# Gate stage as one stream of 8-row blocks, basic block with its bands prepared in stages

## The chip, the cores and the metric

The kernel runs on one core of a Trainium2 chip. The metric is the device time of one execution in microseconds (us); the kernel before takes 7872.17 us, the median of three runs (7866.06 to 7881.12). All data is 32-bit float.

## The reference

Input x has the shape (2, 128, 128, 128): two images (B = 2), 128 channels, 128 rows (H), 128 columns. Four layers follow each other:

- **Layers 0 and 2**: a 3x3 convolution, a small state-space scan (Mamba) over eight tokens of 16 channels at each pixel, a group normalisation, SiLU, and the layer's input added.
- **Layer 1, the density gate**, which the change touches. For each 8x8 window, channel c in a group of 32 gets a density from its distances to the group's channels, then a small network turns the densities into gains, and the gains are interpolated to all pixels:

```
dist(c, d) = |x_c - x_d|^2 over the 64 pixels of the window, c and d in one group
den(c)     = mean over d of exp(-dist / 2)
hid        = relu(w1 den + b1)            # 128 -> 32 channels, one value a window
gain       = 0.5 + sigmoid(w2 hid + b2)   # 32 -> 128 channels, one value a window
out        = x * bilinear_upsample(gain)  # 16x16 windows -> 128x128 pixels, corners aligned
```

- **Layer 3, the basic block**, which the change also touches: relu(x + bn2(conv3x3(relu(bn1(conv3x3(x)))))), with the batch statistics taken over both images, so that each normalisation waits for a whole convolution.

## The kernel before, in words

Channels lie on the 128 partitions. Layers 0 and 2 (`_mamba`) run in an order written out by hand, in which every operation has a due time. They fill 0 to 3320 us and 3640 to 6950 us and are not changed. SiLU and the residual of layer 0 are made at the beginning of the gate stage, those of layer 2 at the beginning of the basic block.

**Gate stage, `_gates`** (3320 to 3640 us). Each image has 16 blocks of 8 rows (`nh`), 32 blocks in all. A block goes through these steps:

- `load`: y and the layer's input, SiLU on ScalarE (L636), residual on GpSimd (L638) into x, window by window.
- `turn`: eight PE transposes (L652) into PSUM (`pt`), copied by VectorE to xt (L654), squared by ScalarE to xq (L656); ScalarE squares x (L659) and VectorE sums the squares per window to nsq (L661, L662).
- `density`: 72 small matmuls, each two instructions (L671, L681), then kk on VectorE (L689), a minimum with 0 on GpSimd (L695), Exp on ScalarE (L696).
- `total`: sums kk (L700).
- `gain`, once for each image after its 16 blocks: two small matmuls, Relu, Sigmoid, + 0.5.
- `apply`: the upsampling as matmuls over 32 rows of contraction (L738), multiplied by x on VectorE (L747), stored from ScalarE's queue (L751).

An image's applies come only after its `gain`, so x of a whole image is held in SBUF (`nh + 5` buffers). The PSUM tiles of turn, gain and apply share two buffers of three banks (`wide`). The order of this stage's instructions is left to the framework's scheduler.

**Basic block, `_basic_block`** (6946 to 7861 us). The 3x3 convolution goes over 32 bands of 8 rows. Four combinations of a band's rows (`combine`: two on GpSimd, L818 and L821, two on VectorE, L819 and L820) are multiplied by transformed weights, which takes twelve matmuls of 512 columns a band, 24 PE instructions (L828). ScalarE copies one product (L836); VectorE forms the two output rows (L839 to L842) and takes statistics (L844). `convolve` prepares one band ahead:

```
v = combine(band(*bands[0]))
for k, at in enumerate(bands):
    ahead = combine(band(*bands[k + 1])) if k + 1 < len(bands) else None
    conv(u, v, *at, stats)
    v = ahead
```

In the first convolution `first` loads a band and the layer's input, applies SiLU (L876), adds the residual on GpSimd (L877) and stores the result, x3, from ScalarE's queue (L878). In the second, `second` takes the rows from SBUF (L900) and copies the two rows that bands share (L894). A closing pass loads x3 (L910), adds (L911), applies Relu (L912) and stores (L913), with three buffers in rotation.

Of the kernel before, what the change touches and what calls it, by code (L numbers as in the profile page):

```python
# [24 lines left out]
F32 = mybir.dt.float32  # L25
# [66 lines left out]
def _place(k):  # L92


    q = k // 2
    return k % 2 + 2 * (q // 4), q % 4


def _upsampling(H):

    _, fy = _bilinear(H)
    ix, fx = _bilinear(P)
    wx = np.zeros((P // WIN, P), np.float32)
    wx[ix, np.arange(P)] = 1.0 - fx
    wx[ix + 1, np.arange(P)] += fx
    segs = _segments(H)
    up = np.zeros((4, 2, P // WIN, 4, max(e - a for _, a, e in segs), P), np.float32)
    for k, a, e in segs:
        n, g = _place(k)
        for h in range(a, e):  # L110
            up[g, 0, :, n, h - a] = (1.0 - fy[h]) * wx
            up[g, 1, :, n, h - a] = fy[h] * wx
    return up.reshape(P, 4, -1)
# [488 lines left out]
def _gates(tc, src, w, con, y, stats, wm, b1, up, dst, H):  # L602

    nc = tc.nc
# [3 lines left out]
    nwin = nh * nw  # L608
    segs = _segments(H)
    with tc.tile_pool(name="dg", bufs=2) as dp, tc.tile_pool(name="dg1", bufs=1) as sp, tc.tile_pool(  # L610
        name="ps_t", bufs=2, space=PSUM
    ) as pst, tc.tile_pool(name="ps_g", bufs=1, space=PSUM) as psg:

        def wide():
            return pst.tile([P, 3 * ROWS, P], F32, tag="pt", name="pt")

        class Small:


            def tile(self, shape, dtype, tag=None, name=None):  # L620
                return wide().rearrange("p a b -> p (a b)")[: shape[0], : shape[1]]

        norm = [_norm(nc, sp, Small(), w, con, stats, b) for b in range(B)]
        ct = sp.tile([P, 4, up.shape[2]], F32, tag="ct", name="ct")

        dens = [sp.tile([P, nh, 2, npair], F32, tag=f"dens{b}", name="dens") for b in range(B)]
        held, live, gains = {}, {}, {}

        def load(b, y0):

            rows = slice(y0 * WIN, (y0 + 1) * WIN)
            g = dp.tile([P, WIN, P], F32, tag="g", name="g", bufs=4)
            nc.sync.dma_start(out=g, in_=y[b][:, rows, :])
            xr = dp.tile([P, WIN, P], F32, tag="xr", name="xr", bufs=4)
            nc.sync.dma_start(out=xr, in_=src[b][:, rows, :])
            nc.scalar.activation(g, g, AF.Silu, bias=norm[b][1], scale=norm[b][0])  # L636
            x = held[b, y0] = dp.tile([P, nw, WIN, WIN], F32, tag="x1", name="x1", bufs=nh + 5)
            nc.gpsimd.tensor_tensor(by_row(x), by_row(xr, False), by_row(g, False), ALU.add)  # L638
# [6 lines left out]

        def turn(b, y0):

            x = held[b, y0].rearrange("p x r w -> p (x r w)")

            pt = wide()[:, :npair, :]  # L650
            for k in range(npair):
                nc.tensor.transpose(pt[:, k, :], x[:, k * P : (k + 1) * P], con["ident"])  # L652
            xt = dp.tile([P, npair, P], F32, tag="xt", name="xt")
            nc.vector.tensor_copy(xt, pt)  # L654
            xq = dp.tile([P, npair, P], F32, tag="xq", name="xq")
            nc.scalar.activation(xq, pt, AF.Square)  # L656

            sq = dp.tile([P, nw, WIN * WIN], F32, tag="sq", name="sq", bufs=1)
            nc.scalar.activation(sq.rearrange("p x r -> p (x r)"), x, AF.Square)  # L659
            nsq = dp.tile([P, nw], F32, tag="nsq", name="nsq")  # L660
            nc.vector.tensor_reduce(nsq, sq, AX.X, ALU.add)  # L661
            nc.vector.tensor_scalar_mul(nsq, nsq, -0.5)  # L662
            live[b, y0] = xt, xq, nsq

        def density(b, y0):
            xt, xq, nsq = live.pop((b, y0))
# [21 lines left out]
            kk = dp.tile([P, 2, npair, CG], F32, tag="kk", name="kk", bufs=3)  # L688
# [8 lines left out]
            live[b, y0] = kk  # L697

        def total(b, y0):
            nc.vector.tensor_reduce(dens[b][:, y0], live.pop((b, y0)), AX.X, ALU.add)  # L700

        def gain(b):

            den = sp.tile([P, nh, npair, 2], F32, tag="den", name="den")
            nc.vector.tensor_scalar_mul(den, dens[b].rearrange("p y a k -> p y k a"), 1.0 / CG)
            p1 = wide().rearrange("p a b -> p (a b)")[:CG, :nwin]
            nc.tensor.matmul(p1, lhsT=wm["w1"], rhs=den.rearrange("p y k a -> p (y k a)"), start=True, stop=True)
            hid = sp.tile([CG, nwin], F32, tag="hid", name="hid")
            nc.scalar.activation(hid, p1, AF.Relu, bias=b1)
            p2 = wide()[:, :4, :]  # L710
            gt = gains[b] = sp.tile([P, 4, P], F32, tag="gain", name="gain")
            for n in range(4):
                at = (n % 2 + n // 2 * WIN) * nw
                m = min(P, nwin - at) // 32 * 32
                if m <= 0:
                    continue
                nc.tensor.matmul(p2[:m, n, :], lhsT=hid[:, at : at + m], rhs=wm["w2"], start=True, stop=False)
                nc.tensor.matmul(p2[:m, n, :], lhsT=wm["one"][:, :m], rhs=wm["b2"], start=False, stop=True)
                nc.scalar.activation(gt[:m, n, :], p2[:m, n, :], AF.Sigmoid)
                nc.vector.tensor_scalar_add(gt[:m, n, :], gt[:m, n, :], 0.5)  # L720

        def apply(b, y0):

            r0 = y0 * WIN
            pu = wide()
            o = dp.tile([P, WIN, P], F32, tag="g", name="o", bufs=4)
            x = by_row(held.pop((b, y0)))

            cut = [a for k, a, _ in segs if k % 2 == 0 and r0 < a < r0 + WIN]
            at = 0  # L730
            for first, end in zip([r0, *cut], [*cut, r0 + WIN]):
                for r in range(first, end, ROWS):
                    for k, a, e in segs:
                        lo, hi = max(a, r), min(e, r + ROWS, end)
                        if lo < hi:
                            n, g = _place(k)
                            q = slice(g * 32, (g + 1) * 32)
                            nc.tensor.matmul(  # L738
                                pu[:, at + lo - first : at + hi - first, :],
                                lhsT=gains[b][q, n, :],  # L740
                                rhs=ct[q, n, (lo - a) * P : (hi - a) * P],
                                start=True,
                                stop=True,
                                tile_position=(q.start, 0),
                            )
                rows = slice(first - r0, end - r0)
                nc.vector.tensor_tensor(  # L747
                    by_row(o[:, rows, :], False), by_row(pu[:, at : at + end - first, :], False), x[:, rows], ALU.mult
                )
                at += (end - first + ROWS - 1) // ROWS * ROWS  # L750
            nc.scalar.dma_start(out=dst[b][:, r0 : r0 + WIN, :], in_=o)  # L751

        order = [(b, y0) for b in range(B) for y0 in range(nh)]
        N = len(order)
        ready = []
        for n in range(-4, N + 2):
            if ready:
                apply(*ready.pop(0))
            if n % 2 == 0:
                for i in range(n + 4, min(n + 6, N)):  # L760
                    load(*order[i])
            if n == -4:
                nc.sync.dma_start(out=ct, in_=up)
            if 0 <= n < N:
                turn(*order[n])
            if 1 <= n <= N:
                density(*order[n - 1])
            if n >= 2:
                b, y0 = order[n - 2]
                total(b, y0)  # L770
                if y0 == nh - 1:
                    gain(b)
                    ready += [(b, i) for i in range(nh)]
        for at in ready:
            apply(*at)


def _basic_block(tc, src, y, norm, x3, w1, w2, bn, out, B, H):
# [6 lines left out]
    with tc.tile_pool(name="bb", bufs=1) as cp, tc.tile_pool(name="bband", bufs=2) as bp, tc.tile_pool(  # L785
# [28 lines left out]
        def combine(xb):  # L814

            v = combined()
            d = [xb[:, k : k + BAND - 1 : 2, :] for k in range(4)]
            nc.gpsimd.tensor_tensor(v[:, 0], d[0], d[2], ALU.subtract)  # L818
            nc.vector.tensor_tensor(v[:, 1], d[1], d[2], ALU.add)  # L819
            nc.vector.tensor_tensor(v[:, 2], d[2], d[1], ALU.subtract)  # L820
            nc.gpsimd.tensor_tensor(v[:, 3], d[1], d[3], ALU.subtract)  # L821
            return v
# [32 lines left out]
        def rest():  # L855
            return bp.tile([P, BAND + 2, P], F32, tag="xs", name="xs", bufs=3)

        bands = [(b, r0) for b in range(B) for r0 in range(0, H, BAND)]

        def convolve(u, band, n):  # L860

# [134 lines left out]
```

## Time and profile before

The profiled execution has a span of 7860.9 us.

| stage | from, us | to, us |
|---|---|---|
| layer 0 without its SiLU and residual | 0 | 3320 |
| gate stage (table load of the first SiLU to the end of the last apply) | 3332.4 | 3634.5 |
| layer 2 without its SiLU and residual | 3640 | 6950 |
| basic block: weights and first bands | 6946 | 6980 |
| basic block: first convolution | 6980 | 7390 |
| basic block: second convolution | 7401 | 7733 |
| basic block: closing pass | 7741 | 7861 |

| engine | busy, us | share of the span |
|---|---|---|
| PE (matmul) | 6537.9 | 83% |
| PEld (weight load) | 2217.4 | 28% |
| DVE (VectorE) | 6831.1 | 87% |
| ACT (ScalarE) | 4291.8 | 55% |
| POOL (GpSimd) | 5521.1 | 70% |

How to read it: the shares are averages over stages with different limits, and layers 0 and 2 make up 84% of the span. For a change in the other two stages they say little; those stages have to be read by themselves. In the lines of the profile, `x<-xr,g` is the tile written and the tiles read; L638 is a line of the kernel before.

### The profile page before, as it was taken

The page shows a single profiled execution, that of the slowest core. Times are in us where ns is not written, and L with a number is a line of the kernel's source. Part 1 is how long each engine was busy: PE and PEld are TensorE (multiplying, and loading weights), DVE is VectorE, ACT ScalarE, POOL GpSimd, SP SyncE. Part 2 cuts the span into 40 slices and gives each one's busy share as a digit, 9 for nine tenths or more (in the row PEclk, how much of TensorE's full clock was granted, in tenths as well). Part 3 has the DMA queues.
Part 4 walks back from the last instruction along what each step waited for, and adds up shares of the span by engine and source line. Part 5 has one row for each costly group of instructions (what it writes and reads, how often), then busy time and mean ns, then how long its engine had stood idle before and what let it go on. Part 6 is the DMA issues. An engine that isn't in the chain of part 4 may idle for free. (4 is left out here: it accounts for less than half of the span.)

```text
span 7860.9 us, 86792 instructions
## 1 busy us (share of the span) xinstructions
PE 6537.9 (83%) x29412; PEld 2217.4 (28%) x29412; DVE 6831.1 (87%) x6360; ACT 4291.8 (55%) x4835; POOL 5521.1 (70%) x1810
## 2 busy tenths in 40 slices
PE   7888888888888888777888888888888888878893
PEld 2222222222222222253222222222222222223341
DVE  5999999999999999863999999999999999963454
ACT  5656666666666656482665665666656656621112
POOL 5777887777778777652777778787777777843330
PEclk8999999999999999866999999999999999979996
DMA  7999999999999999854999999999999999955204
GB/s 203 246 243 246 253 249 247 253 250 256 249 248 254 245 249 248 225 179 127 244 249 246 250 250 251 252 251 253 252 239 249 250 250 250 250 157 139 69 0 163
DMA packets 573435, 1765.42 MB, mean 225 GB/s; under 512 B 85536, under 2 KB 239680, under 8 KB 458176
## 3 DMA queue, kind: packets, MB, share of 16 engines
q1 hardware_dynamic: 530496, 1709.54, 84.0%
q10 hardware_dynamic: 42496, 50.34, 1.8%
q8 instruction: 234, 3.83, 0.2%
q14 instruction: 209, 1.71, 0.1%
HBM read 1549.82 MB, written 209.72 MB: 224 GB/s over the span
## 5 line engine op out<-in xcount | busy, mean ns | idle before, releaser
L451 POOL TENSOR_TENSOR h<-ur,bcr 128x2048 f32<-128x2048 f32 x896 | 4060.4, 4539 | 1193.2 <-DMA bcr<-sb 1006.0
L478 DVE TENSOR_TENSOR set<-set,h 128x1024 f32<-128x1024 f32 x1792 | 2193.0, 1224 | 301.6 <-ACT set L469 216.2
L479 DVE TENSOR_TENSOR r<-set,bcr 128x1024 f32<-128x1024 f32 x1792 | 2194.1, 1224 | 61.4
L469 ACT ACTIVATE set<-set 128x1024 f32<-128x1024 f32 x1792 | 1745.6, 1006 | 868.7 <-PE set L460 854.2
L483 DVE TENSOR_TENSOR h<-set,h 128x1024 f32<-128x1024 f32 x1536 | 1864.5, 1214 | 21.3 <-POOL h L451 21.2
L460 PE MATMUL set<-dt,rep 32*128 32x512 f32 x7168 | 1400.2, 674 | 96.8 <-DVE h L483 89.9
L498 PE MATMUL ys<-r,ct 128*32 128x512 f32 x7168 | 1166.1, 632 | 36.4 <-DVE r L479 36.0
L328 PE MATMUL one<-band,conv 128*128 128x512 f32 x2304 | 1085.5, 607 | 24.6 <-DMA band<-in_x_dram 12.2
L828 PE MATMUL m<-comb,u 128*128 128x512 f32 x1536 | 689.1, 610 | 88.5 <-DVE Y L842 53.2
L406 PE MATMUL one<-xc,keep 128*64 128x512 f32 x1024 | 324.6, 717 | 471.4 <-ACT xc L363 361.5
L460 PEld LDWEIGHTS set<-dt,rep 32*128 32x128 f32 x7168 | 405.2, 193 | 992.7 <-issue 466.2
L328 PEld LDWEIGHTS one<-band,conv 128*128 128x128 f32 x2304 | 408.2, 190 | 674.4 <-issue 599.2
L489 PE MATMUL ys<-t,ct 128*128 128x512 f32 x512 | 326.4, 724 | 252.4 <-DVE v L511 250.9
L357 ACT ACTIVATE xc<-one,keep 128x512 f32<-128x512 f32 x256 | 176.1, 688 | 519.5 <-PE one L355 514.7
L498 PEld LDWEIGHTS ys<-r,ct 128*32 128x32 f32 x7168 | 181.2, 111 | 928.5 <-issue 760.7
L828 PEld LDWEIGHTS m<-comb,u 128*128 128x128 f32 x1536 | 296.6, 195 | 480.3 <-issue 457.3
L426 PE MATMUL one<-prod,ct 128*128 128x512 f32 x512 | 290.3, 650 | 123.1 <-POOL prod L418 88.8
L380 POOL TENSOR_TENSOR u<-dt,xc 128x1024 f32<-128x1024 f32 x128 | 302.8, 2366 | 70.7 <-ACT dt L374 70.6
L355 PE MATMUL one<-y,w_in 128*128 128x512 f32 x512 | 343.5, 759 | 5.8 <-ACT xc L357 3.1
L469 ACT ACT_TABLE_LOAD x252 | 323.3, 1283 | 4.6
L370 PE MATMUL one<-xc,w_dt 128*128 128x512 f32 x512 | 313.5, 696 | 4.1 <-ACT bc L413 4.1
L427 ACT COPY t<-one 128x512 f32<-128x512 f32 x256 | 150.2, 587 | 301.4 <-PE one L426 301.4
(136 smaller groups left out, 5894.0 us busy)
## 6 DMA issues: line engine op xcount, KB each, us to landing
ur<-su SPq DMA_DIRECT2D x896, 896.0 KB, 11.5
bcr<-sb SPq DMA_DIRECT2D x896, 448.0 KB, 11.6
ur<-su SPq DMA_DIRECT2D x896, 128.0 KB, 11.1
su<-u SPq DMA_DIRECT2D x1024, 64.0 KB, 3.5
sb<-bc SPq DMA_DIRECT2D x256, 224.0 KB, 2.8
bcr<-sb SPq DMA_DIRECT2D x896, 64.0 KB, 10.9
y<-o SPq DMA_DIRECT2D x128, 256.0 KB, 9.2
band<-in_x_dram SPq DMA_DIRECT2D x28, 640.0 KB, 10.9
```

The source lines that it names most:

```text
L328: nc.tensor.matmul(py.rearrange("p (r w) -> p r w", r=ROWS), lhsT=w["conv"][:, tap, :], rhs=xb[:, r + kh : r + kh + ROWS, kw : kw + P], st ...
L355: nc.tensor.matmul(p, lhsT=w[("in", "z")[i]][:, g, :], rhs=s["y"], start=True, stop=True)
L406: nc.tensor.matmul(p[g * NQ * DS : (g + 1) * NQ * DS, :], lhsT=w[("xb", "xcm")[i]], rhs=s["xc"][:, g, :], start=True, stop=True,)
L451: nc.gpsimd.tensor_tensor(b, s["ur", t], s["bc", t][:, 0].unsqueeze(1).to_broadcast([P, NJ, NS]), ALU.mult)
L460: nc.tensor.matmul(a[j // 2][:, j % 2, :], lhsT=w["rep"][r, q, :], rhs=s["dt"][r, g, :], start=True, stop=True, tile_position=(r.start, 0),)
L469: nc.scalar.activation(x, x, AF.Exp)
L478: nc.vector.tensor_tensor(pt, pt, s["h", t - 1][:, js, :], ALU.mult)
L479: nc.vector.tensor_tensor(s["r", t][:, js, :], pt, s["bc", t - 1][:, 1].unsqueeze(1).to_broadcast([P, 2, NS]), ALU.mult)
L483: nc.vector.tensor_tensor(s["h", t][:, js, :], pt, s["h", t][:, js, :], ALU.add)
L489: nc.tensor.matmul(s["ys", g], lhsT=con["ident"], rhs=s["t1"][:, g, :], start=True, stop=False)
L498: nc.tensor.matmul(s["ys", g][a : a + NQ * DJ, :], lhsT=red[:, q, :], rhs=r[:, j, :], start=False, stop=(q == NQ - 1), tile_position=(0, a),)
L828: nc.tensor.matmul(m[:, i], lhsT=u[:, i, kw, :], rhs=v[:, i, :, kw : kw + P], start=(kw == 0), stop=(kw == 2),)
```

## The change

**Gate stage.** A row of gains needs only the window rows above and below it, so a block can be finished as soon as the hidden values of its neighbours are there. The change makes one stream of all 32 blocks, in which each step works on an older block: turn on block n, density on n - 1, total on n - 2, the first matmul with Relu (`hide`) on n - 3, the second with Exp (`gate`) on n - 5, the rest of the sigmoid (`gain`) and the upsampling matmuls (`spread`) on n - 6, `apply` and the store (`keep`) on n - 7. The sigmoid is made as 1 / (1 + exp(-z)), so that Exp is the only other table beside SiLU. The upsampling takes four window rows at once, 64 rows of contraction for each half of the block, with weights laid out by block (4 MB instead of 2.3 MB). PSUM tiles of turn and spread have two banks; two buffers are shared by both. The order is now that of the program, on all engines, and stores go through SyncE's queue.

**Basic block.** Bands lie in three rooms whose borders are cleared once. `convolve` loads three bands ahead, makes (SiLU and residual, or Relu) two ahead, and combines one ahead. All four combinations are on GpSimd. The closing pass rotates four buffers: two as before and the two of the combinations.

```diff
 def _gates(tc, src, w, con, y, stats, wm, b1, up, dst, H):
...
-            x = held[b, y0] = dp.tile([P, nw, WIN, WIN], F32, tag="x1", name="x1", bufs=nh + 5)
+            s["x"] = dp.tile([P, nw, WIN, WIN], F32, tag="x1", name="x1", bufs=14)
...
-            pt = wide()[:, :npair, :]
+            pt = pst.tile([P, npair, P], F32, tag="pt", name="pt")
...
+        def hide(b, y0):
+            p = psg.tile([CG, nw], F32, tag="one", name="ph")
+            nc.tensor.matmul(
+                p, lhsT=wm["w1"], rhs=live[b, y0].pop("den").rearrange("p a k -> p k a"), start=True, stop=True
+            )
+            nc.scalar.activation(hidden[b][:, y0 + 1, :], p, AF.Relu, bias=b1, scale=1.0 / CG)
+
+        def gate(b, y0):
+            s = live[b, y0]
+            p = psg.tile([P, P], F32, tag="one", name="pz")
+            h = hidden[b][:, y0 : y0 + 4, :].rearrange("p y x -> p (y x)")
+            for a in range(0, P, P // 2):
+                nc.tensor.matmul(p[a : a + P // 2, :], lhsT=h, rhs=wm["w2"], start=True, stop=False)
+                nc.tensor.matmul(p[a : a + P // 2, :], lhsT=wm["one"], rhs=wm["b2"], start=False, stop=True)
+            s["e"] = dp.tile([P, P], F32, tag="e", name="e")
+            nc.scalar.activation(s["e"], p, AF.Exp, scale=-1.0)
+
+        def gain(b, y0):
+            e = live[b, y0]["e"]
+            nc.vector.tensor_scalar_add(e, e, 1.0)
+            nc.vector.reciprocal(e, e)
+            nc.vector.tensor_scalar_add(e, e, 0.5)
+
+        def spread(b, y0):
+            s = live[b, y0]
+            pu = s["pu"] = pst.tile([P, 2 * ROWS, P], F32, tag="pt", name="pu")
+            for n in range(2):
+                q = slice(n * P // 2, (n + 1) * P // 2)
+                nc.tensor.matmul(
+                    pu[:, n * ROWS : (n + 1) * ROWS, :].rearrange("p r w -> p (r w)"),
+                    lhsT=s["e"][q, :],
+                    rhs=weights[q, y0, :],
+                    start=True,
+                    stop=True,
+                )
...
+        stages = ((0, turn), (1, density), (2, total), (3, hide), (5, gate), (6, gain), (6, spread), (7, apply), (7, keep))
+        E = mybir.EngineType
+        with tc.manual_schedule(engines={E.PE, E.Activation, E.DVE, E.Pool, E.SP}):
+            for n in range(-6, N + 8):
+                if n % 2 == 0:
+                    for m in range(max(n + 4, 0), min(n + 6, N)):
+                        load(*order[m])
+                    for m in range(max(n + 2, 0), min(n + 4, N)):
+                        residual(*order[m])
+                for lag, stage in stages:
+                    if 0 <= n - lag < N:
+                        stage(*order[n - lag])
 
 def _basic_block(tc, src, y, norm, x3, w1, w2, bn, out, B, H):
...
-            nc.gpsimd.tensor_tensor(v[:, 0], d[0], d[2], ALU.subtract)
-            nc.vector.tensor_tensor(v[:, 1], d[1], d[2], ALU.add)
-            nc.vector.tensor_tensor(v[:, 2], d[2], d[1], ALU.subtract)
-            nc.gpsimd.tensor_tensor(v[:, 3], d[1], d[3], ALU.subtract)
+            d = [xb[:, n : n + BAND - 1 : 2, :] for n in range(4)]
+            for i, (m, n, op) in enumerate(((0, 2, ALU.subtract), (1, 2, ALU.add), (2, 1, ALU.subtract), (1, 3, ALU.subtract))):
+                nc.gpsimd.tensor_tensor(v[:, i], d[m], d[n], op)
...
-            return bp.tile([P, BAND + 2, P], F32, tag="xs", name="xs", bufs=3)
+            return bp.tile([P, BAND + 2, P], F32, tag="xs", name="xs")
...
+            v = {}
+            for k in range(-3, len(bands)):
+                for ahead, f in ((3, load), (2, make)):
+                    if 0 <= k + ahead < len(bands):
+                        f(k + ahead)
+                if 0 <= k + 1 < len(bands):
+                    v[k + 1] = combine(k + 1)
+                if k >= 0:
+                    conv(u, v.pop(k), *bands[k], stats)
...
-        for b, r0 in bands:
-            xr = rest()[:, :BAND, :]
+        for k, (b, r0) in enumerate(bands):
+            if k % 2 == 0:
+                xr = rest()[:, :BAND, :]
+            else:
+                xr = combined().rearrange("p a b c -> p (a b c)")[:, : BAND * P].rearrange("p (r w) -> p r w", r=BAND)
```

## The prediction

> **What bounds the kernel now.** I read four views, in this order: busy time by stretch (cut where the timeline shows a stage begin or end), the waits, the timeline of one block, the groups by form. Columns of the first: stretch, its length, then busy time (and instructions) of PE, PEld, DVE, ACT and POOL, the granted TensorE clock, DMA share, GB/s.
>
> ```profile
> 3332.00:3448.00 116.00, 65.50 (x2592) 53.20 (x2592) 68.13 (x86) 111.28 (x106) 72.75 (x37) 0.71 0.63 218
> 3448.00:3560.00 112.00, 99.03 (x2225) 63.30 (x2225) 76.92 (x97) 66.61 (x71) 47.49 (x26) 0.69 0.39 138
> 3560.00:3635.00 75.00, 66.85 (x259) 33.45 (x259) 26.04 (x34) 4.11 (x8) 2.24 (x2) 0.51 0.29 117
> 6980.00:7390.00 410.00, 356.27 (x768) 150.19 (x767) 159.25 (x249) 61.99 (x62) 164.13 (x129) 0.95 0.49 133
> 7401.00:7733.00 332.00, 331.54 (x768) 145.55 (x766) 185.14 (x249) 55.59 (x62) 111.63 (x127) 0.99 0.00 0
> 7741.00:7860.00 119.00, 0.00 (x0) 0.00 (x0) 40.96 (x33) 36.61 (x32) 0.00 (x0) 0.50 0.79 269
> ```
>
> Rows one to three are the gate stage: 302 us from its first table load (3332.4) to the end of its last apply (3634.5), 9.4 us for each of 32 blocks. ScalarE bounds its first part (111 of 116 us), PE at half clock its last. Row four is the first 3x3 convolution: 410 us for the 768 PE instructions that the second (row five) does in 332 us, with PE busy throughout. So 78 us of it are waiting. Row six is the closing pass: no PE, DMA at 79%.
>
> Waits of the first convolution (who <- releaser: us, times, longest):
>
> ```profile
> ACT band L876 <- DMA band<-y: 237.8, 30, 16.8
> DVE Y L839 <- ACT m L836: 233.2, 30, 9.0
> ACT m L836 <- POOL band L877: 82.3, 25, 3.8
> PE m L828 <- DVE Y L842: 53.2, 25, 3.9
> PE m L828 <- DVE comb L819: 24.8, 1, 24.8
> ```
>
> PE waits for DVE; DVE waits for the copy L836; that copy stands in ScalarE's queue behind the x3 store, which waits for GpSimd's residual L877, for SiLU, for a band loaded one band ahead.
>
> For the gates I ask what may overlap. From the timeline of one block (start, length, instruction, idle before it):
>
> ```profile
> 3513.44 1.23 DVE L654 COPY xt<-pt 128x1024 f32<-128x1024 f32 x1 [1.98 <-PE pt L652]
> 3514.70 1.02 ACT L656 ACTIVATE xq<-pt 128x1024 f32<-128x1024 f32 x1 [2.93 <-DVE xt L654]
> 3515.62 1.05 ACT L659 ACTIVATE sq<-x 128x1024 f32<-128x1024 f32 x1
> ```
>
> The square xq reads the same PSUM tile as the copy xt, yet starts 0.03 us after xt's end, after ScalarE had idled 2.93 us. So the two readers are ordered, not parallel.
>
> Durations, from the groups by form of the gate stage:
>
> ```profile
> L638 POOL TENSOR_TENSOR x<-xr,g 128x1024 f32<-128x1024 f32 x32 | 75.4, 2361 | 80.9 <-DMA g<-y 40.8 <-ACT g L636 13.9 <-DVE o L747 10.5
> L695 POOL TENSOR_SCALAR kk<-kk 128x512 f32<-128x512 f32 x32 | 47.6, 1486 | 70.0 <-DVE kk L689 64.8 <-DVE gain L720 5.2
> L661 DVE TENSOR_REDUCE nsq<-sq 128x16 f32<-128x1024 f32 x32 | 38.9, 1216 | 32.6 <-ACT sq L659 31.9
> L636 ACT ACTIVATE g<-g,aff_t,aff_s 128x1024 f32<-128x1024 f32 x32 | 38.9, 1236 | 0.8 <-DMA g<-y 0.5
> L689 DVE TENSOR_TENSOR kk<-pg,nsq 128x512 f32<-128x512 f32 x32 | 22.0, 687 | 17.9 <-PE pg L681 17.5
> L700 DVE TENSOR_REDUCE dens<-kk 128x16 f32<-128x512 f32 x32 | 21.8, 680 | 8.8 <-ACT kk L696 8.8
> L696 ACT ACTIVATE kk<-kk 128x512 f32<-128x512 f32 x32 | 20.2, 630 | 25.3 <-POOL kk L695 25.1
> ```
>
> **What the Trainium skill says.** "TensorE: Matmul & The Clock Gate", specification table: ScalarE, VectorE and GpSimd queues are strict FIFO, TensorE's can only pull weight loads ahead. The trace agrees (L836 behind the x3 store), and my forecast rests on it. The same page, Part 1: the PE clock halves after an idle window of about 3.4 us and returns after a busy one. Rows one to three agree: 0.71, 0.69, 0.51. "GPSIMD Engine Reference", specification table: GpSimd shares SBUF with VectorE, and VectorE instructions with two SBUF inputs contend. The trace agrees: the combination on DVE takes 0.68 us at its quickest and 1.82 us, the median of the second convolution, beside GpSimd's.
>
> **The gates, part by part.** The new order is written by hand: in iteration n each engine's queue holds, in this order, turn(n), density(n-1), total(n-2), hide(n-3), gate(n-5), gain(n-6), spread(n-6), apply(n-7). With FIFO queues that gives a closed loop:
> - transposes T(n) on PE, then xt(n) on DVE 1.22, xq(n) on ScalarE 1.01 (ordered, see above), sq(n) behind it 1.05, nsq(n) on DVE 1.22, its scaling 0.17 (median);
> - kk(n-1) behind that on DVE 0.69, the min on GpSimd 1.49, Exp 0.63;
> - hide's Relu(n-3) behind that Exp on ScalarE. It reads 32x16; taken 0.20, from the 128x1 square root at 0.20;
> - gate(n-5) on PE: its PSUM tile has the tag "one" with a single buffer, which hide's tile holds until that Relu;
> - spread(n-6) behind gate on PE, then T(n+1) behind spread. The loop is closed.
>
> Outside PE: 1.22 + 1.01 + 1.05 + 1.22 + 0.17 + 0.69 + 1.49 + 0.63 + 0.20 = 7.7 us, and about 0.5 us for hand-overs (PE to DVE 0.25 as T to xt; the rest 0.03 to 0.09). On PE, full clock and half: T, eight transposes, 1.1 and 2.0. Gate is eight instructions; four such of L717/L718 took 1.2 us, with twice the columns; so 1.3 and 2.2. Spread is four instructions of 512 columns: 0.427 us each in the second convolution, 0.85 at half, with start-up 1.9 and 3.6. PE idles some 5 us in each loop (from the end of density to gate), so it starts cold and warms later: I take 1.6 + 1.7 + 2.9 = 6.2, between 4.3 and 7.8. The loop is 14.4 us, from 12.5 to 16.0.
>
> Density, 2.2 us, lies beside xt to nsq. SiLU of two blocks with its table load, 3.8 us every second iteration, and GpSimd's residuals, 4.7, lie beside spread, T and xt. The new reciprocal has no row of its shape; it lies between 0.22 (the tensor-scalar L720 of that shape, by its median) and five times that, an upper bound that I choose. Either way total 0.68, three gain operations and an occasional stall by GpSimd take under 3 us, beside the 4.5 us from the min to the end of gate: nothing. Sigmoid's three table loads go (3.8 us).
>
> Sum: iterations 0 to 5 have no spread; the loop there is xt to kk plus total, 6.3 us, or 10.3 with the two SiLUs: with 5 us of lead, 53. Iterations 6 to 31: 26 x 14.4 = 374. The drain, iteration 32 and six of gate and spread: 33. Together 460, against 302: **+158**. The new weights table is 4 MB instead of 2.3, ahead of the first loads; 2.3 MB landed in 8.8 us, so 6.8 more, half of it hidden behind the norm: **+3**. The row stores move from ScalarE's queue to SyncE's; behind a store waiting for apply stand loads needed two iterations later: nothing.
>
> **The basic block.** All four combinations go to GpSimd: 4 x 1.29 (its uncontended median) + residual 2.68 = 7.9 us a band, under PE's 332 / 32 = 10.4. Loading three bands ahead hides the 5.5 us landing, and SiLU, residual and x3 store come before the copy L836 needs its turn. The first convolution should then run as the second: 410 - 332 = **-78**. The second is PE-bound and stays. GpSimd's first two combinations at each start cost 2 x 1.29 instead of about 1.8: **+1.5** over both. The closing pass rotates four buffers instead of three: load 4.3, DVE 1.3, ACT 1.2, store 3.6 make about 10.5 us, /3 = 3.5 as now, /4 = 2.6; but DMA at 269 GB/s is 79% busy, so 340 GB/s caps 1.05 MB a band at 3.1. I take 3.25 for 32 bands, 104 for 119: **-15**.
>
> Net: 158 + 3 - 78 + 1.5 - 15 = +69.5; 7872 + 69.5 = 7941.
>
> **Rivals.** (A) The lags decouple the engines and the busiest bounds the stage. DVE would have 5.9 to 6.8 us a block, ACT 5.7. 32 x 6.5 + 25 for both ends is 233: -69, net -158, 7714. For it: nearly every stage reads an older block. Against: the FIFO loop above. (B) The loop closes over total and gain instead of min, Exp, Relu and gate (the "one" buffer binds less than I read), and PE stays warmer: 14.4 - 2.8 = 11.6, 26 x 11.6 + 86 = 388: +86, net about 0, 7872. Against: the single buffer in the code. (C) The gates as forecast, but the convolution keeps its waits: GpSimd at the contended 1.75 gives 9.7 us a band, and the order on ScalarE's queue still holds up L836. Gain 20 instead of 78: 7999. Against: no VectorE instruction with two SBUF inputs is left there.
>
> **How the numbers follow.** Forecast 0.56, A 0.12, B 0.15, C 0.13; the rest, 0.04, is wider still. The loop's bounds give 26 x 12.5 and 26 x 16.0, with the ends 76 to 95: 401 to 511, net 7880 to 7992. The range takes in these and B: 7860 to 7993. It leaves out A and C's upper end. Faster: A, and a third of B: 0.17. Same (within 16 us): the middle of B and the forecast's low end: 0.08. Slower: 0.75.
>
> **What would show it.** Right: applies 12 to 16 us apart in mid-stage; DVE, ACT and POOL each under 60% there; PE's gate waiting for Relu, transposes right behind spread; the first convolution at about 332 us. Wrong: DVE or ACT near 95% in the gates (A), gate starting before that block's Exp (B), or the first convolution above 370 us with L836 still waiting for GpSimd (C).

## The result and the profile after

The changed kernel takes 7986.98 us (median of four runs, 7969.65 to 8003.9) against 7876.65 us of the kernel before beside it: 1.014 times as long, 95% interval 1.011 to 1.0169. The forecast was 7941, slower; the time lies in its range (7860 to 7993).

The profiled spans, 7967.9 and 7860.9 us, differ by 107.0 us. By stages, each taken from its first to its last instruction (the last apply of the kernel before ends at 3633.6 us, not at 3634.5, which makes its gate stage 301.2 us):

| stretch | before, us | after, us | difference | forecast |
|---|---|---|---|---|
| up to the first SiLU of the gate stage | 3332.4 | 3327.9 | -4.5 | +3 |
| gate stage | 301.2 | 416.3 | +115.1 | +158 |
| from there to the first convolution (layer 2) | 3346.1 | 3339.2 | -6.9 | 0 |
| first convolution | 409.8 | 423.2 | +13.4 | -78 |
| between the convolutions | 10.6 | 12.7 | +2.1 | +1.5 (both starts) |
| second convolution | 332.5 | 332.6 | +0.1 | 0 |
| to the closing pass | 8.4 | 8.4 | -0.1 | 0 |
| closing pass | 120.0 | 107.5 | -12.5 | -15 |

Two terms of the forecast are far off, and they partly cancel: the gate stage lost 43 us less than I said, the first convolution gained nothing of its 78 us. Busy time by stretch of the kernel after (length; busy time and instructions of PE, PEld, DVE, ACT, POOL; clock; DMA share; GB/s), for the gate stage, the two convolutions and the closing pass:

```profile
3328.00:3744.00 416.00, 233.89 (x5312) 150.35 (x5312) 203.18 (x288) 173.05 (x222) 122.39 (x64) 0.64 0.32 119
7084.00:7507.00 423.00, 354.73 (x768) 149.41 (x766) 116.70 (x186) 60.28 (x61) 224.66 (x160) 0.95 0.48 127
7519.00:7852.00 333.00, 332.61 (x768) 146.16 (x768) 116.79 (x186) 54.06 (x60) 158.79 (x159) 0.99 0.01 2
7860.00:7967.00 107.00, 0.00 (x0) 0.00 (x0) 40.89 (x34) 36.51 (x32) 0.00 (x0) 0.50 0.84 294
```

In the gate stage no engine is busy for more than 56% of the time, and the DMA share is 0.32; ScalarE has fallen from 96% (111 of 116 us in the first part before) to 42%. Something other than the busiest engine sets the pace, and the timeline shows it. One iteration of the kernel after, weight loads and DMA left out:

```profile
3553.95 1.23 DVE L648 COPY xt<-pt 128x1024 f32<-128x1024 f32 x1 [4.35 <-PE pt L646]
...
3555.27 1.02 ACT L650 ACTIVATE xq<-pt 128x1024 f32<-128x1024 f32 x1 [4.93 <-DVE xt L648]
...
3556.19 1.05 ACT L653 ACTIVATE sq<-x 128x1024 f32<-128x1024 f32 x1
3557.27 1.22 DVE L655 TENSOR_REDUCE nsq<-sq 128x16 f32<-128x1024 f32 x1 [2.09 <-ACT sq L653]
...
3558.61 0.68 DVE L683 TENSOR_TENSOR kk<-pg,nsq 128x512 f32<-128x512 f32 x1
...
3559.38 1.48 POOL L689 TENSOR_SCALAR kk<-kk 128x512 f32<-128x512 f32 x1 [11.37 <-DVE kk L683]
...
3560.90 0.63 ACT L690 ACTIVATE kk<-kk 128x512 f32<-128x512 f32 x1 [3.66 <-POOL kk L689]
...
3561.43 0.25 ACT L703 ACTIVATE hid<-ph,b 32x16 f32<-32x16 f32 x1
3561.73 0.69 PE L711 MATMUL pz<-w,hid 32*64 32x128 f32 x4 [5.42 <-ACT hid L703]
...
3562.21 0.64 PE L712 MATMUL pz<-w 32*64 32x128 f32 x4
3562.79 2.08 PE L729 MATMUL pu<-up,e 64*128 64x512 f32 x4
...
3564.80 1.97 PE L646 MATMUL pt<-ct,x 128*128 128x128 f32 x8
...
3566.80 1.22 DVE L648 COPY xt<-pt 128x1024 f32<-128x1024 f32 x1 [4.35 <-PE pt L646]
```

Read from top to bottom, each line begins within 0.3 us of the end of the one above it, and the last is the first of the next block: 3566.80 - 3553.95 = 12.85 us. It is the loop of the prediction, link by link. The applies stand 12.6 to 13.1 us apart through the whole middle of the stage.

The first convolution waits as it did before. Waits of the kernel after in that stretch (who <- releaser: us, times, longest):

```profile
DVE Y L838 <- ACT m L835: 301.8, 30, 22.3
ACT band L886 <- DMA band<-y: 243.2, 29, 10.9
PEld m L827 <- POOL comb L820: 90.3, 30, 5.0
ACT m L835 <- POOL band L887: 78.9, 24, 3.3
PE m L827 <- DVE Y L841: 67.9, 26, 4.2
```

ScalarE still waits 243 us for bands that are now loaded three ahead. The timeline of one band says why (SPq and ACTq are the entries in which SyncE and ScalarE issue a DMA):

```profile
7202.99 0.37 SPq L878 DMA_DIRECT2D band<-y  x1
7208.03 1.46 ACT L886 ACTIVATE band<-band,aff_t,aff_s 128x1280 f32<-128x1280 f32 x1 [8.52 <-DMA band<-y]
7209.56 2.67 POOL L887 TENSOR_TENSOR band<-band,xs 128x1280 f32<-128x1280 f32 x1 [6.60 <-ACT band L886]
7212.19 4.64 POOL L820 TENSOR_TENSOR comb<-band 128x520 f32<-128x520 f32 x4
7212.27 0.42 ACTq L888 DMA_DIRECT2D x<-band  x1
7212.81 0.59 ACT L835 COPY m<-m 128x512 f32<-128x512 f32 x1 [3.32 <-PE m L827]
...
7216.05 10.54 PE L827 MATMUL m<-comb,u 128*128 128x512 f32 x24 [3.34 <-DVE Y L841]
7216.86 0.37 SPq L878 DMA_DIRECT2D band<-y  x1
```

Counting the instructions from the stage's first gives their bands. The load, SiLU, residual and x3 store are of band 12; the combinations behind them are of band 10, and the copy L835 of band 8. In the source, the combinations of band 10 stand ahead of the residual of band 12, and the copy of band 8 ahead of SiLU and store of band 12. The basic block is not under the hand-written order; the framework's scheduler placed them so. The room of band 13 comes free when the combinations of band 10 end (7216.83), and only then is it loaded. So one loop runs through load 5.0, SiLU 1.5, residual 2.7 and combinations 4.6: 13.8 us for this band (in mid-stage these loads stand 12.7 to 14.8 us apart), against 10.4 that PE needs (332.6 over 32 in the second convolution).

### The profile page after: what moved, and what is told of

Its sections match the earlier page's. It is cut to its first block, busy times and chain, and to the rows that moved or that the text cites. A ratio compares the mean times of both kernels' runs of the same rounds, so it can differ in the third digit from the quotient of the medians.

```text
span 7967.9 us, 87195 instructions
## 1 busy us (share of the span) xinstructions
PE 6541.0 (82%) x29648; PEld 2213.3 (28%) x29648; DVE 6745.4 (85%) x6304; ACT 4281.0 (54%) x4873; POOL 5628.9 (71%) x1879
## 5 line engine op out<-in xcount | busy, mean ns | idle before, releaser
L838 DVE TENSOR_TENSOR Y<-m,m 128x512 f32<-128x512 f32 x64 | 44.0, 688 | 528.1 <-ACT m L835 528.1
L820 POOL TENSOR_TENSOR comb<-band 128x520 f32<-128x520 f32 x256 | 298.1, 1197 | 165.3 <-PE m L827 161.9
## 6 DMA issues: line engine op xcount, KB each, us to landing
ur<-su SPq DMA_DIRECT2D x896, 896.0 KB, 11.5
```

The lines of the kernel that those rows point to most:

```text
L820: nc.gpsimd.tensor_tensor(v[:, i], d[m], d[n], op)
```

## The experiments

Times are medians; the ratio is to the kernel before, measured beside each run, with its 95% interval. The kernel before took 7869.70 us beside e1 to e4, 7881.64 beside e5 to e8 and 7858.19 beside e9.

| run | time, us | ratio | gate stage | first convolution | closing pass |
|---|---|---|---|---|---|
| e1_old_gates | 7876.36 | 1.0006 (0.9992 to 1.0019) | 302.9 | 422.2 | 107.5 |
| e2_block_in_order | 7890.95 | 1.0029 (1.0019 to 1.0038) | 414.5 | 331.7 | 106.3 |
| e3_later_two | 7950.49 | 1.0093 (1.0067 to 1.0119) | 373.8 | 422.9 | 110.1 |
| e4_old_gates_block | 7778.28 | 0.9887 (0.9865 to 0.9909) | 301.4 | 331.9 | 107.6 |
| e5_two_buffers | 7966.15 (one run) | | 413.1 | 422.7 | 107.4 |
| e8_later_one_buffer | 7985.92 (one run) | | 415.1 | 426.2 | 109.3 |
| e6_reorder | 7922.61 | 1.0050 (1.0032 to 1.0067) | 331.6 | 423.6 | 110.0 |
| e7_split_combine | 7803.61 | 0.9896 (0.9873 to 0.9919) | 305.8 | 332.4 | 109.5 |
| e9_seven_buffers | 7755.76 | 0.9864 (0.9835 to 0.9892) | 296.7 | 332.1 | 78.4 |

Stages are from each profiled execution. The unchanged layers vary from one execution to the next: the first SiLU of the gates stands between 3328 and 3362 us in the profiles of the changed kernel and of these nine. So stages say more than single totals.

**e1: the old gate stage with the new basic block.** `_gates` and its tables as in the kernel before, the rest as changed.

> The gate stage of the kernel before with the changed basic block. If the two parts add, the gate stage takes 302 us again instead of 418, and what is left of the change is a first convolution of 423 us instead of 410 and a closing pass of 108 instead of 120: 7870 to 7885, the kernel before within 0.2%. Rival: the changed block profits or suffers from the gate stage before it (clock, buffers), then over 7900 or under 7855.

Measured: 302.9 us of gates, 422.2 and 107.5 us in the block, and no difference in time. The whole loss is the gate stage's; the basic block's change is worth nothing as it stands, its lost 13 us paid by the closing pass.

**e2: the bands in program order.**

```diff
             v = {}
-            for k in range(-3, len(bands)):
-                for ahead, f in ((3, load), (2, make)):
...
+            E = mybir.EngineType
+            with tc.manual_schedule(engines={E.PE, E.Activation, E.DVE, E.Pool, E.SP}):
+                for k in range(-3, len(bands)):
+                    for ahead, f in ((3, load), (2, make)):
...
```

> The changed kernel, but the bands of both convolutions keep the program's order on every engine. Theory: in the changed kernel the framework put the residual of band k + 2 ahead of the combinations of band k on GpSimd, and SiLU and x3 store of band k + 4 ahead of the copy of band k on ScalarE, so that one loop goes through load 4.9, SiLU 1.5, residual 2.7 and combinations 4.6, 13.7 us a band. In program order the loop spans two bands and PE bounds: the first convolution 330 to 345 us instead of 423, the kernel about 85 us faster than the changed one, 7895 to 7915. Rival: GpSimd's sum or the landing of the bands is the bound in itself; then the first convolution stays above 400 us and the time near 7985.

Measured: the first convolution falls from 423.2 to 331.7 us. The time, 7890.95 us, is 4 us below the expected 7895 to 7915. Nothing but the order differs: the loads, combinations and buffers are the same. Its row by stretch, and one band of its timeline:

```profile
7102.00:7434.00 332.00, 331.73 (x768) 145.83 (x768) 116.73 (x186) 57.11 (x61) 225.78 (x161) 0.99 0.52 164
```

```profile
7258.87 0.59 ACT L835 COPY m<-m 128x512 f32<-128x512 f32 x1 [8.47 <-PE m L827]
7259.35 1.46 ACT L888 ACTIVATE band<-band,aff_t,aff_s 128x1280 f32<-128x1280 f32 x1
...
7260.94 2.68 POOL L889 TENSOR_TENSOR band<-band,xs 128x1280 f32<-128x1280 f32 x1 [3.38 <-issue]
7263.57 4.66 POOL L820 TENSOR_TENSOR comb<-band 128x520 f32<-128x520 f32 x4
...
7268.25 0.37 SPq L880 DMA_DIRECT2D band<-y  x1
```

PE is busy throughout. SiLU (L888) follows the copy with no wait for a band, and GpSimd idles 3.38 us a band, with 225.8 us of work in 332. GpSimd was not the bound, and neither was the landing of the bands.

**e3, e5 and e8: which link holds gate.** e5 gives gate's PSUM tile a tag of its own; e8 puts gate, gain, spread and apply one block later; e3 does both.

```diff
-            p = psg.tile([P, P], F32, tag="one", name="pz")
+            p = psg.tile([P, P], F32, tag="two", name="pz")
...
-        stages = (..., (5, gate), (6, gain), (6, spread), (7, apply), (7, keep))
+        stages = (..., (6, gate), (7, gain), (7, spread), (8, apply), (8, keep))
```

> The changed kernel with gate, gain, spread and apply one block later and a PSUM buffer of its own for gate. Theory: gate then waits for no Relu of its own iteration, and the loop closes over total and the gain operations instead of min, Exp, Relu and gate: about 11.3 us instead of 12.8, so 26 x 1.5 = 40 us less, one drain step more: 7940 to 7955. Rival: the loop is bound by the PSUM buffers of turn and spread alone; then it stays at 12.8 us and the time within 10 us of the changed kernel.

> The changed kernel with a PSUM buffer of its own for gate, nothing else. The prediction held that gate waits for the Relu because the two share one buffer. If that is the link, the loop falls from 12.8 to about 11.5 us. Rival: gate of block n - 5 reads the hidden values of block n - 3 anyway, which that same Relu writes; then the loop stays at 12.8 us.

> The changed kernel with gate, gain, spread and apply one block later, nothing else: gate reads only hidden values of earlier iterations, but still shares one buffer with hide. If data alone was the link, the loop falls to about 11.5 us; if buffer and data are links side by side, it stays within 0.3 us of 12.8, and only both together (11.5 us measured) help.

Measured: in mid-stage the applies stand 12.6 to 13.1 us apart with the buffer of its own (e5), except two steps of 11.5; 12.7 to 12.9 with the later lag (e8); 11.1 to 11.5 with both (e3, whose 7950.49 us lie in the expected range). So two links lie side by side, and either alone holds gate back: the shared buffer that the prediction named, and the data. Gate of block n - 5 reads the hidden values of four rows, the last of which is that of block n - 3, which the same iteration's Relu writes. The two short steps of e5 fit this: they belong to the last two blocks of the first image, for which block n - 3 is in the other image, so that no data link is left, and in both of them gate starts before that iteration's Relu (at 3561.91 and 3572.92 us, with Relu at 3567.09 and 3578.63).

The data link is one that the kernel doesn't need: in `_upsampling` the row index `y - y0 + 1` takes the values 0, 1 and 2 for all 128 rows of the image, never 3, so the weights of the fourth row are zero throughout. Gate waits for a row that is then multiplied by zero. A gate that reads three rows and has a buffer of its own should do what e3 does without the later lag; no run tried it.

With both links gone the loop closes where the expectation said, over the gain operations. Waits of e3 in mid-stage (us, times, longest):

```profile
PE pu L729 <- DVE e L721: 104.9, 24, 5.1
```

Spread, which in the kernel after came straight behind gate, now waits for the last gain operation, 24 times.

**e6: another order of the same instructions.**

```diff
-        stages = ((0, turn), (1, density), (2, total), (3, hide), (5, gate), (6, gain), (6, spread), (7, apply), (7, keep))
+        stages = ((6, gain), (0, turn), (3, hide), (1, density), (2, total), (5, gate), (6, spread), (7, apply), (7, keep))
```

> The changed kernel with the same lags, buffers and instructions in the gate stage, but another order in an iteration: gain, turn, hide, density, total, gate, spread, apply. Theory: strict queues close the loop, so order alone decides; with gain and hide ahead, their chain no longer stands behind kk and Exp, and spread need not wait for gain. By the same durations the loop becomes about 9.7 us: gate stage 320 to 335 us instead of 416, time 7885 to 7910. Rival: the sum of the work on PE and its half clock binds the stage; then the stage stays above 390 us.

Measured: the stage falls from 416.3 to 331.6 us, as expected; the loop alternates between 9.2 and 10.4 us. The time, 7922.61, is above the expected 7885 to 7910. In its profile, which is of its slowest run (7930.74), the layers 0 and 2, which are the same code, took 43 us more than in that of the kernel after (3357.2 and 3353.0 against 3327.9 and 3339.2); no run shows why. Timeline of an iteration of e6:

```profile
3544.83 0.25 ACT L703 ACTIVATE hid<-ph,b 32x16 f32<-32x16 f32 x1
...
3545.13 0.44 PE L711 MATMUL pz<-w,hid 32*64 32x128 f32 x4 [0.88 <-ACT hid L703]
...
3545.72 1.13 PE L729 MATMUL pu<-up,e 64*128 64x512 f32 x4
...
3546.30 0.69 DVE L683 TENSOR_TENSOR kk<-pg,nsq 128x512 f32<-128x512 f32 x1
...
3547.49 1.22 DVE L740 TENSOR_TENSOR o<-pu,x 128x1024 f32<-128x1024 f32 x1
3548.59 0.63 ACT L690 ACTIVATE kk<-kk 128x512 f32<-128x512 f32 x1 [3.51 <-POOL kk L689]
3548.86 1.94 PE L646 MATMUL pt<-ct,x 128*128 128x128 f32 x8 [2.01 <-DVE o L740]
```

Relu, gate and spread now come before kk and the Exp of their iteration. The loop that is left closes over a PSUM buffer: the transposes wait for apply, which frees it. That is still 30 us more than the old stage.

**e4 and e7: the old gates with the basic block in program order; in e7 two of the combinations are back on VectorE.**

```diff
-                nc.gpsimd.tensor_tensor(v[:, i], d[m], d[n], op)
+                (nc.vector if i in (1, 2) else nc.gpsimd).tensor_tensor(v[:, i], d[m], d[n], op)
```

> The gate stage of the kernel before and the basic block in program order. If both theories hold and add: 302 us of gates, 335 us for each convolution, 108 us of closing pass: 7785 to 7800, faster than both kernels by 1%. If the block's gain does not appear, 7870 to 7885.

> The gate stage of the kernel before and the basic block in program order, with two of the four combinations back on VectorE as before. If the order is what matters, PE still bounds: both convolutions at 332 us, and the time within 0.3% of the kernel with all four on GpSimd (7778). If moving them to GpSimd was needed, contention between the two engines lengthens VectorE's combinations to 1.8 us and the first convolution to over 345 us.

Measured: e4 takes 0.9887 of the kernel before, faster than both kernels and a little below its expected 7785. e7's convolutions take 332.4 and 331.6 us, and its ratio, 0.9896, lies within the interval of e4. The contention that its expectation names is there (VectorE's combinations took up to 1.79 us in the first convolution), but PE's work hides it. Here it doesn't matter which engine makes two of the combinations once the order is right.

**e9: e4 with seven buffers in the closing pass.** The rooms of the bands, idle by then, join the rotation.

```diff
-            if k % 2 == 0:
+            if k % 7 in (0, 3):
                 xr = rest()[:, :BAND, :]
+            elif k % 7 in (2, 4, 6):
+                xr = room[k % 7 // 2 - 1].rearrange("p a b -> p (a b)")[:, : BAND * P].rearrange("p (r w) -> p r w", r=BAND)
```

> The gate stage of the kernel before, the basic block in program order, and a closing pass that rotates seven buffers (two as before, the two of the combinations, the three band rooms). The prediction held that three buffers bound the closing pass by the round trip of a buffer and that with four the DMA does. If so, seven give little over four: the pass falls from 108 to 100 to 106 us and the kernel by under 8 us, 7770 to 7785. Rival: the round trip still binds with four; then seven take it below 95 us.

Measured: 78.4 us, not 100 to 106, so the rival was right: with four buffers the round trip of a buffer still bound the pass. The closing pass of e4 (four buffers; below its row, what SyncE's loads of x3 waited for) and of e9 (seven):

```profile
7697.00:7803.00 106.00, 0.00 (x0) 0.00 (x0) 40.35 (x33) 36.62 (x32) 0.00 (x0) 0.50 0.85 297
SPq L932 <- DMA out_dram<-comb: 59.4, 14, 5.6
SPq L932 <- DMA out_dram<-xs: 34.3, 14, 13.2
```

```profile
7672.00:7750.00 78.00, 0.00 (x0) 0.00 (x0) 40.80 (x34) 36.39 (x32) 0.00 (x0) 0.50 0.95 383
```

With four buffers 28 of the 32 loads waited for the store of the band that had the buffer before them; the other four had been issued ahead of the pass. Seven buffers also let seven bands land ahead of the pass instead of four, so that 29.9 instead of 31.5 MB are moved within it. By the two rates that is 4 to 5 us (an estimate); the rest of the 29 us is the pace.

This kernel, at 0.9864 of the kernel before, has the lowest ratio of the study. Its interval overlaps that of e4 (0.9887), so the step from four to seven buffers is seen in the stage, not in the totals.

## Why the prediction was right where it was, and where it was not

- **Direction and range: right, the range by 6 us.** The gate stage outweighs all else, as forecast. e1 shows that it is the whole loss: with the old stage the difference is gone. But the median, 7986.98, is just under the range's upper end, and two of the four runs (7997.48 and 8003.9) are above it.
- **The gate loop: the mechanism right, its size too large.** The links stand in the profile as listed. The term that was mis-sized is PE's share, "1.6 + 1.7 + 2.9 = 6.2": transposes took 2.0 to the copy, gate 1.06, spread 2.01, 5.1 in all. Not because PE became warm: over all three the granted clock was 0.50, and at half clock the prediction had 2.0 + 2.2 + 3.6 = 7.8. It counted the instructions of gate and spread as one behind the other, and they run two at a time. Each of spread's four takes 1.05 to 1.22 us, yet the four take 2.08; the trace starts them in pairs, 6 ns apart. Spread's two products use different halves of the 128 rows of contraction, gate's two write different halves of its output. The rest of the loop was 7.8 us, against 8.2. 26 loops x (14.4 - 12.85) = 40 of the 43 us. (One sum of the prediction is short: three loops of 6.3 and three of 10.3 us with 5 of lead make 54.8, not 53.) The clock by stretch (gate, spread, transposes) and spread's instructions (ns, shortest/median/longest):

```profile
3561.70:3562.80 1.10, 1.07 (x10) 0.74 (x10) 0.75 (x1) 0.00 (x0) 0.00 (x0) 0.50 0.00 0
3562.80:3564.80 2.00, 2.00 (x7) 0.50 (x5) 0.00 (x0) 1.86 (x3) 0.00 (x0) 0.50 0.81 266
3564.80:3566.80 2.00, 2.00 (x18) 1.67 (x24) 0.00 (x0) 2.00 (x2) 0.92 (x1) 0.50 0.95 313
L729 PE MATMUL pu<-up,e x128: 1054/1122/1219, 3396.1 to 3741.9; 64*128 64x512 f32 x128
```
- **The clock was read too simply.** That PE "starts cold and warms later" is not what this stretch shows, and spread's instructions took over 1.05 us throughout the stage, where full-clock ones of 512 columns take 0.59. Nor do all three rows of the gate stage before agree with a clock that returns after a busy window: in the third PE is busy for 67 of 75 us at a granted clock of 0.51. What the clock follows there stays open.
- **One link was named by half.** "Its PSUM tile has the tag 'one' with a single buffer" is true and binds (e8), but e5 shows that it isn't alone; the data of block n - 3 is a second link of the same length.
- **Rival B** had its 11.6 us loop right for a kernel with both links removed (11.1 to 11.5 in e3), but the change isn't that kernel.
- **Rival A: false.** DVE is busy 49% and ACT 42% of the stage. The lags between stages decouple little here while older blocks' work stands behind newer blocks' in the same queue. e6 shows that order alone is worth 85 us.
- **The first convolution: wrong.** The step that failed is "Loading three bands ahead hides the 5.5 us landing, and SiLU, residual and x3 store come before the copy L836 needs its turn. The first convolution should then run as the second". I read the order from the source, where the gates rightly were read so; but the basic block has no hand-written order, and the program's queues differ from its text. The runs showed 423.2 us, and 331.7 with the order alone put right (e2). Rival C named the symptom, the copy held behind the store, but gave GpSimd's contention as half of its reason; with no work of VectorE beside them GpSimd's four combinations took 4.64 us, a little under the 4 x 1.29 forecast.
- **The closing pass: the size nearly right, the reason wrong.** -12.5 us against -15. But "340 GB/s caps" does not hold: e9 moved 383 GB/s, and the pass fell by another 29 us. The step that failed is the round trip of "about 10.5 us", taken as the same with four buffers. In mid-pass of e4 it was 13.5 to 14.4 us from the issue of a load to the landing of its store, so 3.5 us a band over four buffers, and not 2.6; in e9 17.2 to 17.7, 2.5 over seven.
- **The 4 MB table: not seen.** The first SiLU came 4.5 us earlier, within what layer 0 varies by.

The two errors, 43 us too much and 91 us too little, went against each other, so the net forecast of +69.5 looks better than its parts. That it came within 40 us of the measured 107 is luck. What happened is the waiting convolution of rival C with a gate loop shorter than forecast; C with the gates as forecast was 7999, outside the range.

What stays open: why the scheduler put the residual ahead of the combinations. The two buffers of the combinations are a candidate, since combine(k) has to wait for the convolution of band k - 2, but no run tried it. Whether order alone would repair the first convolution of the kernel before, with its single band of lookahead, wasn't tried either.

## What to carry to other kernels

A software pipeline over in-order queues can be no faster than the longest loop that order, buffers and data close, however idle its engines: write down, for one iteration, what stands behind what on each engine, and look for a path that comes back to its start. Where a scheduler sets the order, read it from the profile (count which block each instruction belongs to) before giving a stage more lookahead; here 91 us came with the order alone, the buffers being the same. Check too what an instruction reads: a tile that it doesn't need is a wait all the same. Before calling a streaming pass bound by the DMA, add buffers: here a share of 0.79 to 0.85 was not the limit.

## What the runs showed of the hardware that I had not expected

- DMA busy share isn't in proportion to bytes: 269 GB/s at 0.79, 297 at 0.85, 383 at 0.95. Scaling the first to a full share gave 340, and the pass went well over it.
- The reciprocal of 128x128 elements took 0.95 us on VectorE, four times a tensor-scalar of that shape (0.23 to 0.27).
- GpSimd's four combinations are not alike: in the kernel after, the first and the last, which it made before too, take 1.28 to 1.31 us, as before (1.29 at the median), and the two that came over from VectorE 1.09 to 1.11. With VectorE's two beside them (e7, first convolution) the first and the last take 1.74 us at the median.
- Two matmuls on different halves of the rows of contraction ran at the same time: spread's four instructions of 1.05 to 1.22 us took 2.08.
